# One softmax per query tile, more copies on ScalarE, and a new order of pieces in a gated cross-attention and local-attention block

## The chip, the cores and the metric

The kernel runs on one core of a Trainium2 chip. The metric is device time in microseconds, the median of several runs; lower is better. The core has five instruction queues that run side by side: TensorE (PE) for matmuls, VectorE (DVE), ScalarE (ACT), GpSimd (POOL), and SyncE (SP), which issues transfers. Each queue runs its own instructions in order. Where one needs what another queue produces, it waits on a semaphore.

## The reference

The input is `x` of shape (8, 256, 128): eight sequences of 256 tokens, 128 wide. First comes a gated cross-attention to a context of the same shape (16 heads of 8), then six layers on the residual stream, then a second gate. All arithmetic is in float32.

```python
x = x + tanh(g_xattn) * xattn(layernorm(x), ctx, ctx)      # 16 heads of 8, softmax over 256 keys
h = layernorm(x)
for i in range(6):
    h = attn_layer(shift_tokens(h), Wqkv[i], q_scale[i], k_scale[i], Wo[i]) + h
    h = ffn_layer(shift_tokens(h), ln_g[i], ln_b[i], W1[i], b1[i], W2[i], b2[i]) + h
x = x + tanh(g_ffn) * h

# attn_layer: 16 heads of 64
q, k, v = split(x @ Wqkv)
q, k = l2norm(q) * qs, l2norm(k) * ks
q = q*cos*scale + rotate_half(q)*sin*scale ;  k likewise with 1/scale
# windows of 32 queries see their own 32 keys and the 32 before: 64 keys
sim  = where(mask, -max, q k^T * 8)
attn = softmax(sim) ;  out = (attn @ v) @ Wo

# ffn_layer
xn = (x - mean) / sqrt(var + 1e-5) * g + b
a, gate = split(xn @ W1 + b1) ;  return (a * gelu(gate)) @ W2 + b2
```

## The kernel before

**Tiling.** A sequence is two tiles of 128 tokens on the 128 partitions. `st[b]` is the residual stream of sequence b, features on partitions and tokens along the row, with one column in front for the token shift. There are 6 x 8 = 48 passes through `sequence(k, l, b)`, k = 8 l + b, layer after layer.

**One pass.** Queries and keys of the two tiles make four *chunks* c (CHUNKS: tile 0 key, tile 0 query, tile 1 key, tile 1 query), each in two halves of 512 columns. For each half, `project` (L544, `proj{c}{half}`) does the matmul into a PSUM tile `pj`; `square` (L552, `sq`) on ScalarE writes squares for the norm; `rotate` (L560, `rot`) on VectorE multiplies `pj` with the cosine and sine tables. `squares_sum` (L569, `ss`) sums the squares; `rotate_add` (L575, `radd`) on GpSimd adds the two rotated halves; `norms` and `norms_inverse` (L583 to L591, `norms`, `ninv`) make inverse norms; `normalize` (L598, `nrm`) on GpSimd applies them; `qk_transpose` (L608, `pqt`) and `qk_evacuate` (L616, `qe`) turn queries and keys. Values go by `v_project` (L623, `vp`) and `v_evacuate` (L631, `ve`).

`scores` (L644, `sc{t}{i}`) gives a [128, 16 heads, 64 keys] tile of tile t in PSUM. The softmax works on *groups* of eight heads: four groups, each in two parts. `maxima` (L660, `mx`) does one fused operation per head: mask added, negative minimum taken, result to SBUF. `exponentials` (L670, `ex`) does one activation per head, with the maximum as bias and the row sum accumulated. `sums_inverse` (L679, `rs`) and `divide` (L685, `div`, on GpSimd) finish a group. `p_transpose` (L703, `pt`), `p_evacuate` (L712 and L714, `pe{t}{x}`, on VectorE but for the one piece named in `P_ON_SCALAR`) and `corners` (L720, `co`) turn the probabilities. `attend` (L741) multiplies with the values in two phases, `at` and `aw`; `between` (L752, `av`) is a small VectorE read that lets phase 1 start only when phase 0 is complete. `o_evacuate` (L755, `oe`), `o_project` (L764, `wo`) and `o_add` (`oadd`) end the attention.

The feed-forward half: `f_transpose` (L777, `ftr`), `f_stats` (L194 to L197, `fst`: statistics, then variance plus epsilon), `f_rstd` (L201, `frs`, a power on GpSimd), `f_norm` (L205, `fno`), `f_back` (L793, `fba`), `f_affine` (L798, `faf`), `f_up` (L813; `fga` for the gate half, `fva` for the value half), `f_gelu` (L820, `fge`), `f_gate` (L826, `fgt`), `f_down` (L837, `fdo`) and `f_add` (`fad`).

**The cross-attention** (`cross(b)`, pieces whose names begin with x) runs once per sequence, ahead of that sequence's first layer and beside the layers of earlier sequences. `stats_of` and its epsilon step serve it too.

**What sets the order.** There is no scheduler. Each piece is recorded with a time, `k * SLOTS + PLAN[piece]` with SLOTS = 5; all pieces of all passes are sorted by that time and emitted in that order, and that is the order of every queue. The pieces of one pass have times from 0 to 22.6, so the pieces of some five passes lie interleaved, and after the start the same order repeats for every k. `CROSS_SHIFT` moves each cross block.

```python
    def at(k, piece, fn, *args):
        time = PLAN[piece] if isinstance(piece, str) else piece
        pieces.append((k * SLOTS + time, len(pieces), fn, args))
```

**Buffers.** PSUM has three pools of two buffers each: `ps_p` (tiles pj, pv, px and the cross tiles of tag "pj"), `ps_s` (pqt, scores s, ppt2, po, the gate tile pga) and `ps_m` (ppt1, pa, pw, pxt). In SBUF, the squares tile `sq` has one buffer, the rotation product `ur` two, `u` four. A tile that is read by two engines is read by them one after the other, in the order of the pieces.

**Transfers.** SP loads the weights of a layer in one piece (`load`), long before they are used, with two buffers, so a layer's weights arrive while the layer before runs; `load_vectors`, the inputs of the cross blocks and the results are the other transfers. ScalarE issues a few small ones at the start.

## Time and profile before

| | |
|---|---|
| runs | 1791.76 us median of 3 (1790.74 to 1793.51) |
| profiled execution | span 1786.5 us, TensorE clock 0.996 |
| DVE, slice by slice (tenths) | 3 5 4 6 6 6 8, then 9 to the last two slices |
| ACT, slice by slice | 3 3 4 3 4 5 8, then 9 |
| POOL, slice by slice | 3 0 2 2 3 3 6, then 6 to 7 |
| transfers | 26.32 MB, mean 15 GB/s; the 16 engines are 5.3% busy |
| chain that ended last | PE 74%, DVE 17%, ACT 4%, issue 3% |

In the groups of the profile a row gives line, engine, operation, output and input by the program's names, shapes and count; behind the first bar the busy time and the mean ns of one; behind the second the idle time of that engine in front of these instructions and who ended it. Consecutive instructions of one engine overlap a little, so a mean is longer than the distance from start to start, which a timeline shows.

Two stretches can be told apart. Up to some 300 us the cross blocks run, and no engine is full. After that the six layers repeat one pattern to near the end.

Some rows that the change touches:

| line | what | count | mean ns |
|---|---|---|---|
| L660 | masked minimum of one head, 128x64, DVE | 1536 | 213, and 80 to read the result |
| L670 | exponential of one head, 128x64, ACT | 1536 | 342, and 195 to read the sum |
| L679 | reciprocal of 8 sums, DVE | 192 | 195 |
| L685 | division of 8 heads, 128x512, POOL | 192 | 1043 |
| L712 | probability copy 128x512, DVE | 192 | 678 |
| L714 | probability copy 64x1024, DVE and ACT | 48 each | 1206 and 1010 |
| L798 | affine step, 128x256, DVE | 48 | 529 |
| L197 | variance plus epsilon, 128x2, DVE | 64 | 792 |

### The profile page before, as it was taken

Reading aid. Unit: us, or ns where it says so; the run is one execution under the profiler, and the core shown is the slowest. Engines: PE = TensorE matmul, PEld = TensorE weight load, DVE = VectorE, ACT = ScalarE, POOL = GpSimd, SP = SyncE. Lnnn points to the kernel's source line nnn. Section 1 sums busy time; section 2 is a strip of 40 time slices with the busy share of each in tenths; the row PEclk is TensorE's granted clock in tenths of the full one; section 3 lists DMA queues with packets and bytes.
Section 4 is the critical chain, followed back from the end, with each engine's and each line's share of the span. In section 5 each row is a group of like instructions: output and inputs, shape, how many; then the busy total and the mean of one; then the engine's idle time right before and its main releaser. Section 6 shows DMA issues by size and latency. Waiting matters only on the chain.

```text
span 1786.5 us, 78168 instructions
## 1 busy us (share of the span) xinstructions
PE 1724.5 (97%) x32948; PEld 1135.2 (64%) x32948; DVE 1558.6 (87%) x5314; ACT 1487.5 (83%) x4692; POOL 1092.7 (61%) x716
## 2 busy tenths in 40 slices
PE   7999898999999999999999999999999999999997
PEld 4565455666666666666666666666666666666665
DVE  3546668999999999999999999999999999999974
ACT  3343458999999999999999999999999999998984
POOL 3022336767767676776767677676766767676651
PEclk9999999999999999999999999999999999999999
DMA  3000002000011000010000110000100000000000
GB/s 95 7 13 7 7 2 69 3 3 3 3 38 34 3 3 3 3 51 21 3 3 3 39 34 3 3 3 4 50 23 3 3 3 3 3 6 7 6 9 11
DMA packets 34716, 26.32 MB, mean 15 GB/s; under 512 B 16058, under 2 KB 31294, under 8 KB 34366
## 3 DMA queue, kind: packets, MB, share of 16 engines
q1 hardware_dynamic: 33214, 21.20, 4.1%
q8 instruction: 259, 4.24, 1.0%
q14 instruction: 91, 0.75, 0.1%
q10 hardware_dynamic: 1152, 0.14, 0.1%
HBM read 20.28 MB, written 1.05 MB: 12 GB/s over the span
## 4 chain that ended last, share of the span: by engine, by line
PE 74%; DVE 17%; ACT 4%; issue 3%; POOL 0%; DMA 0%; POOLq 0%; ACTq 0%; DVEq 0%
PE pj L544 17%; PE m L764 9%; PE pv L623 9%; PE po L741 8%; PE s L644 7%; PE s L813 5%; PE pw L837 4%; PE pqt L608 4%; DVE ur L560 4%; PE ppt L703 3%; PE pssT L329 3%; DVE x_max L309 3%; DVE squares L569 3%; DVE rstd L197 2%; PE pa L813 2%
## 5 line engine op out<-in xcount | busy, mean ns | idle before, releaser
L598 POOL TENSOR_TENSOR u<-u,rn 128x1024 f32<-128x1024 f32 x192 | 361.3, 1903 | 283.3 <-DVE rn L591 283.3
L575 POOL TENSOR_TENSOR u<-ur 128x1024 f32<-128x1024 f32 x192 | 451.3, 2362 | 127.4 <-DVE ur L560 98.3
L670 ACT ACTIVATE pr<-pr,nmax 128x64 f32<-128x64 f32 x1536 | 513.1, 342 | 0.6
L544 PE MATMUL pj<-w_qkv,st 128*128 128x512 f32 x768 | 409.4, 615 | 5.1 <-ACT x_big L355 2.2
L552 ACT ACTIVATE sq<-pj 128x512 f32<-128x512 f32 x384 | 227.9, 594 | 89.7 <-PE pj L544 66.7
L670 ACT ACTIVATION_READ_ACCUMULATOR pr<-pr,nmax 128x1 f32 x1536 | 299.2, 195 | 0.0
L560 DVE TENSOR_TENSOR ur<-pj,rotk 128x1024 f32<-128x1024 f32 x192 | 234.9, 1224 | 67.7 <-ACT sq L552 60.9
L685 POOL TENSOR_TENSOR pr<-pr,rs 128x512 f32<-128x512 f32 x192 | 198.2, 1043 | 102.6 <-DVE rs L679 102.6
L660 DVE CUSTOM_DVE_ANT_0 pr<-s,mask 128x64 f32<-128x64 f32 x1536 | 234.4, 213 | 14.0 <-PE s L644 10.8
L560 DVE TENSOR_TENSOR ur<-pj,rotq 128x1024 f32<-128x1024 f32 x192 | 231.4, 1205 | 9.9 <-ACT sq L552 8.5
L569 DVE TENSOR_REDUCE squares<-sq 128x16 f32<-128x1024 f32 x192 | 232.2, 1210 | 0.7
L623 PE MATMUL pv<-w_qkv,st 128*128 128x512 f32 x384 | 215.7, 643 | 0.0
L764 PEld LDWEIGHTS m<-oT,w_o 128*128 128x128 f32 x768 | 145.6, 190 | 58.9 <-issue 43.5
L544 PEld LDWEIGHTS pj<-w_qkv,st 128*128 128x128 f32 x768 | 132.7, 189 | 78.0 <-issue 36.5
L764 PE MATMUL m<-oT,w_o 128*128 128x256 f32 x768 | 181.7, 380 | 0.0
L741 PEld LDWEIGHTS po<-prT,v 64*64 64x64 f32 x6144 | 130.4, 133 | 72.4 <-DVE ur L560 33.4
L644 PE MATMUL s<-kT,qT 64*32 64x64 f32 x12288 | 166.0, 224 | 6.6 <-issue 3.6
L608 PEld LDWEIGHTS pqt<-ident,u 64*128 64x128 f32 x3072 | 110.4, 139 | 80.2 <-issue 68.4
L644 PEld LDWEIGHTS s<-kT,qT 64*32 64x32 f32 x12288 | 134.2, 105 | 39.7 <-issue 20.4
L741 PE MATMUL po<-prT,v 64*64 64x96 f32 (+1 forms) x6144 | 149.1, 240 | 1.4 <-DVE prT L712 1.4
L631 ACT COPY v<-pv 128x512 f32<-128x512 f32 x192 | 112.5, 586 | 44.4 <-PE pv L623 44.1
L608 PE MATMUL pqt<-ident,u 64*128 64x64 f32 x3072 | 136.4, 228 | 0.3 <-DVE x_max L309 0.3
(116 smaller groups left out, 2817.4 us busy)
## 6 DMA issues: line engine op xcount, KB each, us to landing
w_qkv<-in_L_ffn_Wqkv SPq DMA_DIRECT2D x18, 512.0 KB, 6.5
w_o<-in_L_ffn_Wo SPq DMA_DIRECT2D x6, 512.0 KB, 4.0
w<-in_L_ffn_W SPq DMA_DIRECT2D x6, 341.0 KB, 3.0
xin<-in_x SPq DMA_DIRECT2D x8, 128.0 KB, 2.7
cin<-in_ctx SPq DMA_DIRECT2D x8, 128.0 KB, 2.3
out<-res SPq DMA_DIRECT2D x8, 128.0 KB, 1.8
w<-in_L_ffn_W SPq DMA_DIRECT2D x12, 64.0 KB, 2.0
rotq<-in_c_cos_q SPq DMA_DIRECT2D x6, 64.0 KB, 3.4
```

Source lines behind the costliest of these rows:

```text
L544: nc.tensor.matmul(pj, st[b][:, t * P : (t + 1) * P], w["qkv"][:, o : o + 512], start=True, stop=True,)
L560: nc.vector.tensor_tensor(ur[:, :, half * 512 : (half + 1) * 512].rearrange("p x (h d) -> p x h d", d=DH), pj.unsqueeze(1).to_broadcast([P ...
L569: nc.vector.tensor_reduce(squares[k % 2][:, t, i, :, 0], c_.pop(("sq", c)), AX.X, ALU.add)
L575: nc.gpsimd.tensor_tensor(u.rearrange("p h (two d) -> p h two d", two=2), ur[:, 0], ur[:, 1, :, ::-1, :], ALU.add,)
L598: nc.gpsimd.tensor_tensor(u, u, rn, ALU.mult)
L608: nc.tensor.transpose(pt[:, h, j, :], uf[rows, j * P : (j + 1) * P], ident[rows, rows])
L623: nc.tensor.matmul(pj, st[b][:, t * P : (t + 1) * P], w["qkv"][:, o : o + 512], start=True, stop=True,)
L644: nc.tensor.matmul(pss[n * WIN : (n + 1) * WIN, par, c, :], c_["qT"][rows, c, o : o + WIN], c_["kT"][rows, c, k0 : k0 + KEYS], start=True, ...
L660: nc.vector.tensor_tensor_reduce(probabilities(t)[:, par * NPAIR + c, :], c_["pss", t][:, par, c, :], mask[:, t, :], -1.0, 3e38, ALU.add, ...
L670: nc.scalar.activation(pr[:, col, :], pr[:, col, :], AF.Exp, bias=c_.pop(("nmax", g, c)), scale=-1.0, accum_out=c_["sums", t][:, col : col ...
L741: nc.tensor.matmul(po[par * DH : (par + 1) * DH, x, i, q0:q1], v[rows, t, h * DH : (h + 1) * DH], prT[rows, column[h], 64 * half : 64 * ha ...
L764: nc.tensor.matmul(pm, weights[l]["o"][:, c, :], oT[:, c, :], start=(first and c == 4 * half), stop=(not first and c == 4 * half + 3),)
```

## The change

1. The layers' softmax works on one query tile with all 16 heads at a time, in six operations: `masked` (VectorE, scores plus mask from PSUM to SBUF), `maxima` (VectorE reduction), `subtract` (GpSimd), `exponentials` (ScalarE, one activation of 128x1024), `sums_inverse` (VectorE reduction and reciprocal), `divide` (GpSimd). The pieces are called ma, mx, sub, ex, rs, div, each with t = 0 and 1.
2. `P_ON_SCALAR` names all six probability copies, so they run on ScalarE.
3. The LayerNorm's affine step and the addition of epsilon run on ScalarE.
4. PLAN has new times for all pieces of the passes and of the cross blocks, and new CROSS_SHIFT. In three places (`rot01`, `rot11`, `rot30`) the rotation of a projection now stands before its square; `pj` is no longer popped by `rotate` for that reason. The loads keep their times, and the times of `scale_bias`, `clear` and `scale_tables` get names of their own.

```diff
-CROSS_SHIFT = [0.0000000, -1.8673571, -3.6163960, -4.9323222, -6.8028984, -8.5383167, -10.3450958, -11.8335433]
-LOAD_FIRST, LOAD_AFTER, LOAD_AFTER_CROSS = -17.1923263, 20.96, -18.88
-P_ON_SCALAR = {(0, 0)}
+CROSS_SHIFT = [-0.8036217, -2.3498031, -3.8942305, -5.4451205, -6.9040521, -8.3883736, -9.8516719, -9.8386715]
+P_ON_SCALAR = {(t, x) for t in range(NT) for x in range(3)}
...
+    eps = const.tile([P, 1], F32, name="eps")
+    nc.gpsimd.memset(eps, EPS)
...
-        nc.vector.tensor_scalar(rstd, mv[:, :, 1], EPS, None, ALU.add)
+        nc.scalar.activation(rstd, mv[:, :, 1], AF.Identity, bias=eps)
...
-            pj = c_.pop(("pj", c, half))
+            pj = c_["pj", c, half]
...
-        def maxima(g, i):
-            t, par = GROUPS[g]
-            for c in range(4 * i, 4 * i + 4):
-                nmax = small.tile([P, 1], F32, tag="nmax", name="nmax", bufs=24)
-                c_["nmax", g, c] = nmax
-                nc.vector.tensor_tensor_reduce(
-                    probabilities(t)[:, par * NPAIR + c, :], c_["pss", t][:, par, c, :],
-                    mask[:, t, :], -1.0, 3e38, ALU.add, ALU.min, nmax,
-                )
...
-                nc.scalar.activation(
-                    pr[:, col, :], pr[:, col, :], AF.Exp,
-                    bias=c_.pop(("nmax", g, c)), scale=-1.0,
-                    accum_out=c_["sums", t][:, col : col + 1],
-                )
...
+        def masked(t):
+            pss = c_.pop(("pss", t)).rearrange("p a c k -> p (a c) k")
+            nc.vector.tensor_tensor(
+                probabilities(t), pss,
+                mask[:, t, :].unsqueeze(1).to_broadcast([P, HEADS, KEYS]), ALU.add,
+            )
+        def maxima(t):
+            top = c_["top", t] = small.tile([P, HEADS], F32, tag="top", name="top")
+            nc.vector.tensor_reduce(top, probabilities(t), AX.X, ALU.max)
+        def subtract(t):
+            pr = probabilities(t)
+            top = c_.pop(("top", t)).unsqueeze(2).to_broadcast([P, HEADS, KEYS])
+            nc.gpsimd.tensor_tensor(pr, pr, top, ALU.subtract)
+        def exponentials(t):
+            pr = probabilities(t)
+            nc.scalar.activation(pr, pr, AF.Exp)
+        def sums_inverse(t):
+            rs = c_["rs", t] = small.tile([P, HEADS], F32, tag="rs", name="rs")
+            nc.vector.tensor_reduce(rs, probabilities(t), AX.X, ALU.add)
+            nc.vector.reciprocal(rs, rs)
+        def divide(t):
+            pr = probabilities(t)
+            rs = c_.pop(("rs", t)).unsqueeze(2).to_broadcast([P, HEADS, KEYS])
+            nc.gpsimd.tensor_tensor(pr, pr, rs, ALU.mult)
...
-            nc.vector.tensor_scalar(
-                xnT, c_.pop("pxt").rearrange("p n t -> p (n t)"),
-                ln_g[:, l : l + 1], ln_b[:, l : l + 1], ALU.mult, ALU.add,
+            nc.scalar.activation(
+                xnT, c_.pop("pxt").rearrange("p n t -> p (n t)"), AF.Identity,
+                scale=ln_g[:, l : l + 1], bias=ln_b[:, l : l + 1],
             )
```

Since one period is five units of PLAN, the times modulo 5 give the order that every period repeats. The new order of the pieces that the prediction speaks of, queue by queue (a prime marks a piece of the following pass):

```
PE   at0 at1 aw0 aw1 | proj11 | sc10 sc11 | pqt1 | fdo | proj10 | wo0 wo1 | vp00 | proj20 | pqt0 pqt2 | ftr |
     proj21 | pt0 | sc00 sc01 | pqt3 | vp10 | fba | proj30 | proj31 | fga | pt1 | proj01' | vp01 | fva | proj00' | vp11
DVE  av0 av1 ninv ss0 rot11 ma1 mx1 rot10 rs0 fad ss1 oadd rot20 fst rs1 rot21 fno ss2 ma0 mx0 rot30 rot31 ss3
     rot01' co fgt rot00'
ACT  oe0 oe1 sq11 ex0 qe10 sq10 qe11 ex1 ve00 sq20 qe00 qe01 qe21 qe20 fst(eps) sq21 pe00 pe02 qe31 qe30 ve10 faf
     pe01 sq30 fge sq31 pe12 pe10 pe11 sq01' ve01 norms ve11 sq00'
POOL nrm1 nrm0 nrm2 sub1 radd0 div0 nrm3 frs radd1 div1 radd2 radd3 sub0
```

TensorE's order in a period of the kernel before, in blocks by output: px, ppt, pv, pqt, s, pj, pxt, pqt, s, pj, pv, s (up), ppt, pv, pj, s and pa (up), pj, po, pw, pj, po, s, pj, m, s, pqt, pv, pj, m, pj, pqt.

More of the change, by code (lines that the diff above doesn't have):

```diff
@@ L115, in at @@
     def at(k, piece, fn, *args):
-        time = PLAN[piece] if isinstance(piece, str) else piece
+        time = PLAN[piece]
         pieces.append((k * SLOTS + time, len(pieces), fn, args))
@@ L924, in load @@
         layers[l] = load_layer(l)
[L926 to L929 removed]
+    at(0, "ld0", load, 0)
+    at(0, "ld0", load_vectors)
+    at(0, "scb", scale_bias)
+    at(0, "clr", clear)
     for b in range(B):
         cross(b)
[L932 removed]
     for l in range(DEPTH):
[L934 to L937 removed]
+        at(l * B, "tab", scale_tables, l)
+        if l == 1:
+            at(B - 1, "ld1", load, l)
+        elif l:
+            at((l - 1) * B, "ldn", load, l)
         for b in range(B):
```

48 lines of the change are left out of this document (12 added, 36 removed), and 77 rows, old and new, of the table PLAN.

## The prediction

> **What bounds the kernel now.** I read the page first, then the busy time of each engine by stretches, then the timelines of one period, the waits, and the groups by shape.
>
> ```profile
> PE 1724.5 (97%) x32948; PEld 1135.2 (64%) x32948; DVE 1558.6 (87%) x5314; ACT 1487.5 (83%) x4692; POOL 1092.7 (61%) x716
> PE   7999898999999999999999999999999999999997
> ```
> ```profile
> 744.00:806.00 62.00, 61.61 (x1274) 40.73 (x1273) 59.43 (x210) 57.14 (x186) 43.20 (x26) 1.00 0.13 43
> ```
>
> The second fence is one stretch of 62 us: PE 61.61 us busy, PEld, DVE 59.43, ACT 57.14, POOL 43.20, clock 1.00. Three engines are nearly full, and TensorE has no room at all. A faster VectorE or ScalarE can bring nothing here; only TensorE's own order, or a new wait in its queue, moves the time.
>
> ```profile
> 317.10 0.41 PE L777 MATMUL px<-ident,st 128*128 128x128 f32 x2
> ...
> 756.14 0.44 PE L777 MATMUL px<-ident,st 128*128 128x128 f32 x2
> ...
> 787.49 0.44 PE L777 MATMUL px<-ident,st 128*128 128x128 f32 x2
> ...
> 1697.78 0.44 PE L777 MATMUL px<-ident,st 128*128 128x128 f32 x2
> ```
>
> L777 runs once for each of the 48 sequence-layers. Start to start is 31.36 us, and 44 such periods lie between 317.10 and 1697.78. So the span is 317.1 (head) + 44 x 31.36 + 88.7 (tail) = 1786.5. I price the change per period, then head and tail.
>
> ```profile
> 746.06 0.79 PE s L644 x53
> 746.85 1.05 PE pj L544 x2
> ...
> 752.12 0.86 PE pj L544 x2
> ...
> 755.60 0.61 ACT sq L552
> 756.21 0.02 issue
> 756.24 1.23 DVE ur L560
> ```
>
> This is the chain of waits. A wide matmul costs 0.86 us, but 1.06 behind a block of narrow ones: each step from narrow to wide costs 0.20. And the rotation (L560) starts only when the square (L552) of the same projection is done; the waits say so 94 times:
>
> ```profile
> DVE ur L560 <- ACT sq L552: 69.4, 94, 8.4
> PEld pv L623 <- DVE ur L560: 34.1, 45, 0.8
> ```
>
> The second line is the other half: pj, pv and px share two PSUM buffers, so a projection waits until both readers of an earlier one are done.
>
> ```profile
> L560 DVE TENSOR_TENSOR ur<-pj,rotk 128x1024 f32<-128x1024 f32 x192 | 234.9, 1224 | 67.7 <-ACT sq L552 60.9 <-ACT pr L670 0.5 <-issue 0.3
> L569 DVE TENSOR_REDUCE squares<-sq 128x16 f32<-128x1024 f32 x192 | 232.2, 1210 | 0.7
> L598 POOL TENSOR_TENSOR u<-u,rn 128x1024 f32<-128x1024 f32 x192 | 361.3, 1903 | 283.3 <-DVE rn L591 283.3
> L820 ACT ACT_TABLE_LOAD x47 | 60.3, 1283 | 0.8
> ```
>
> These are the rows that price the new operations.
>
> **The change, as busy time per period.** All from start to start in the timelines. VectorE loses 32 masked minima (four in 0.57 us: 4.6), four reciprocals (0.6), five probability copies (4 x 0.60 + 1.13 = 3.5), the epsilon (0.93) and the affine step (0.46): 10.1. It gains two masks, two maxima, two sums and two reciprocals. None stands in the trace; a mask is nearest to L560 (PSUM in, 128x1024: 1.22), a reduction to L569 (1.21), a reciprocal of 16 columns to L368 (0.25, 0.13 where the next does not wait): 7.6. Bounds: half (a 128x512 reduction, L309, took 0.68) and 10% above. ScalarE loses 32 exponentials (four in 1.33: 10.6) and gains two of 128x1024 (L340, 1.05), five copies (4 x 0.50 + 0.92), affine (0.47, L820's shape) and epsilon (0.27, L583): 5.8. GpSimd gains two subtractions (L598's form, 1.90; at most L575's 2.36) and changes four divisions of 1.04 into two of 1.90: +3.4, to some 25 us. So VectorE goes from 29.7 to 27, ScalarE from 28.6 to 24; GpSimd is nowhere full. The sums say "relief" and decide nothing: what counts is order.
>
> [...] In this trace L569 took 1210 ns and the elementwise L560 1224 on as many elements, so the row decides and I charge no penalty.
>
> **TensorE's own order.** The work is the same; a period falls from 32 blocks to 26, and the steps from narrow to wide from eight to five: -0.60. The stall at L793 (L544 before it took 1.29 from start to start, not 0.86) would go too: -0.43. Without waits a period would be 31.36 - 1.03 = 30.3 us.
>
> **The new waits.** I followed the new piece order queue by queue. Pieces are named as in PLAN. Three pairs now run rotation first (rot01, rot11, rot30), the rest square first, and each second reader waits for the first. Two places cannot hide:
>
> (a) ScalarE's order is sq30, gelu (fge), sq31; vp01 needs proj31's buffer, which is free after rot31, which waits for sq31. From the end of proj30: rot30 1.22, sq30 0.64, table load 1.29, gelus 1.11, sq31 0.60, rot31 1.25 = 6.1 us. TensorE has proj31, fga, pt1, proj01 in between: 0.86 + 1.29 + 1.13 + 1.06 = 4.3. It stands for 1.8 us at least. Behind it, ss3, rot01 and then sq01 must end before proj00: 2.9 us against vp01 and fva, 0.2 + 0.86 + 1.29: another 0.6.
>
> (b) VectorE's order is rot00, av0. rot00 waits for sq00, which ScalarE runs behind ve11, which waits for vp11, TensorE's last piece before at0. From vp11's end: 0.53 + 0.60 + 1.17 + 0.16 + 0.05 = 2.5 us until aw0 may start; at0 and at1 cover 1.47. It stands 1.0 us. Before, av0 came straight behind the gate (L826) and did not wait.
>
> VectorE's queue then makes (a) worse. The whole loop, from the end of proj10 to the next: sq10 0.64; VectorE without a gap rot10 1.14, sum 1.37, fad 0.87, ss1 1.13, oadd 0.87, rot20 1.14, statistics 0.90, sum 1.37, rot21 1.14, fno 0.64, ss2 1.13, mask and maximum 2.38, rot30 1.22 = 15.30, at 15.94. (proj30 was ready at 14.0, by TensorE's pieces, so rot30 is 0.7 late.) Then sq30 to rot31 4.89, at 20.83; ss3 1.05, rot01 1.22, sq01 0.63, at 23.73; proj00 with its exposed load 1.08, vp11 0.86, at 25.67; (b) 2.51, at 28.18; aw0 and aw1 1.47; proj11 1.06, scores 1.58, pqt1 0.64, fdo 1.49, proj10 0.86, at **35.28**. That is +3.92 a period: 44 x 3.92 = +172.5.
>
> In the trace a table load takes 1283 ns (L820) and the first gelu starts 1.30 us after it began. [...]
>
> **Covered.** Subtractions and divisions: sub1 can start at -0.5 on the loop's clock, and in GpSimd's order radd0, div0, nrm3, frs end at 3.8, 5.7, 7.6, 9.1; pt0 wants div0 at 8.3, fno frs at 9.9. If that cover (0.8) goes, fno and all behind it slip one for one. Epsilon on ScalarE hides behind the second sum and rot21; affine ends at 13.8, fga starts at 14.9; the copies of pt1 end at 21.7, at0 starts at 25.7. Weight loads keep their places in SP's queue; scb, clr and tab move by pieces, on queues with room in the head.
>
> **Head and tail.** The cross part gets a new order, with pssx between pssT and pox; one cross block spans 28.6 us now, of which 8.9 are maxima that could hide. Bounds: -40 (five us of each of eight) to +16 (the loop's loss in four early sequences); I take -5. The tail has no projections, so (a) is gone: 0, within -5 and +8.
>
> Sum: 1786.5 + 172.5 - 5 = 1954; the runs' median stands 5.3 above the profiled span, so **1959 us**.
>
> **Rivals.**
> 1. *Fixed waits only* (chance 0.17): VectorE's new operations cost less, so rot30 and rot20 start when their inputs are there. The loop loses 0.7 + 0.25: 34.3, and the time is 1786.5 + 44 x 2.94 - 5 + 5.3 = 1916. For it: half-size rows at 0.68; against it: full-size rows all at 1.2.
> 2. *VectorE slowed* (0.13): GpSimd is busy more of the time beside it; 10% on its 20 us in the loop gives 37.3 and 2047. Against it: these rows were taken with GpSimd at 70%.
> 3. *The relief wins* (0.12), faster: square and rotation do not hold each other in the places named, and TensorE runs at 30.3: 1786.5 - 44 x 1.03 - 5 + 5.3 = 1741. It decides where the path from proj30 to rot31 takes under 4.3 us rather than 6.1, and that from vp11 to av0 under 1.5 rather than 2.5. For it: fewer steps from narrow to wide; against it: 94 waits of L560 for L552.
> 4. Gains and waits cancel (0.03): 1792.
>
> **How the numbers follow.** The forecast has 0.55, by itself 1925 to 2000. With rivals 1 and 2 the range is 1890 to 2050; it leaves out rivals 3 and 4 and the ends, under 0.2. About 0.2% is what the measurement can tell: faster 0.12, same 0.02, slower 0.86.
>
> **What would show it.** Right: TensorE's share falls to some 87%, the period of the f_transpose line is near 35.3, v_project waits for ur and the attention matmuls for seen; sq is followed by a table load, three gelus, sq. Wrong: a TensorE still 97% busy with a period near 30.3; or large waits elsewhere (GpSimd's divisions before the transposes); or VectorE idle long before rot30, which is rival 1.

## The result, and the profile after

The changed kernel takes **2067.23 us** (median of 4 runs, 2061.27 to 2073.06) against 1791.25 us (1788.42 to 1793.51): a ratio of 1.1544, 95% interval 1.1515 to 1.1572. The direction was right, the size was not: 1959 us were forecast, and the range ended at 2050.

The page of the kernel after, busy time and TensorE's row of the span:

```profile
PE 1762.0 (85%) x32948; PEld 1168.2 (57%) x32948; DVE 1442.1 (70%) x2082; ACT 1281.9 (62%) x2068; POOL 1257.3 (61%) x717
PE   5899888888888888888888888888888888888887
```

TensorE went from 97% to 85%, and no other engine is over 70%: the engines wait for each other. The f_transpose line (L769 now) gives the period again, from the timeline of after:

```profile
323.60 0.44 PE L769 MATMUL px<-ident,st 128*128 128x128 f32 x2
...
1974.30 0.44 PE L769 MATMUL px<-ident,st 128*128 128x128 f32 x2
```

(1974.30 - 323.60) / 44 = **37.52 us** a period, where 35.28 was forecast. The head is 323.6 (312.1 forecast), the tail 2067.1 - 1974.3 = 92.8 (88.7 forecast). The miss is 44 x 2.24 = 98.6 from the loop, 11.5 from the head, 4.1 from the tail, and -5.1 because these runs stand 0.1 above the profiled span and not 5.3. Together that is 109 us, and 108 were measured: the prediction's 44 x 31.36 is 0.9 short of the 1380.7 us between its two rows.

Busy time by engine in the 44 periods, by stretches, after and then before (length, PE, PEld, DVE, ACT, POOL, granted clock):

```profile
323.60:1974.30 1650.70, 1413.22 (x28091) 941.64 (x28089) 1213.41 (x1681) 1083.78 (x1718) 1108.61 (x583) 0.96 0.03 10
```
```profile
317.10:1697.80 1380.70, 1371.31 (x28091) 910.56 (x28089) 1315.87 (x4628) 1272.79 (x4138) 957.11 (x583) 1.00 0.04 12
```

VectorE and ScalarE are relieved nearly as priced: 102 and 189 us less in the loop, where 44 x 2.5 = 110 and 44 x 4.8 = 211 were said. TensorE has the same 28091 matmuls, but is busy 42 us longer, at a clock of 0.96. It is idle for 237.5 us, 5.4 a period; before, it was idle for 9.4 us in the whole loop. The waits of TensorE, after (sum, times, longest):

```profile
PE pv L622 <- DVE ur L559: 87.4, 44, 2.6
PE po L733 <- DVE seen L744: 46.6, 45, 1.2
PE s L641 <- issue: 46.0, 48, 1.8
PE pj L543 <- DVE ur L559: 31.8, 42, 1.1
...
PE pqt L607 <- issue: 14.3, 14, 1.6
```

v_project for the rotation, attention for `seen`: the two places of the prediction. "issue" is idle time in which nothing is waited for that the profile shows; it stands in the run of scores and in the transposes pqt behind them, some 60 us in all, and the prediction had nothing there. One period of TensorE's timeline, after:

```profile
822.10 0.90 PE L641 MATMUL s<-kT,qT 64*32 64x64 f32 x40 [1.34 <-issue]
...
834.51 1.12 PE L622 MATMUL pv<-w_qkv,st 128*128 128x512 f32 x2 [1.63 <-DVE ur L559]
...
837.45 1.13 PE L543 MATMUL pj<-w_qkv,st 128*128 128x512 f32 x2 [0.53 <-ACT sq L551]
...
841.94 1.55 PE L733 MATMUL po<-prT,v 64*64 64x96 f32 x64 [1.03 <-DVE seen L744]
...
856.78 1.13 PE L543 MATMUL pj<-w_qkv,st 128*128 128x512 f32 x2 [0.76 <-DVE ur L559]
```

These are vp01, proj00, aw0 and proj21, with the gap in the scores ahead of them. The chain of waits, after, in front of vp01 (start, length, what):

```profile
828.29 1.24 DVE ur L559
...
829.61 0.60 ACT sq L551
...
830.23 1.28 ACT L812
831.51 0.01 issue
831.52 1.19 ACT hid L812 x3
832.71 0.49 ACT sq L551
```

rot30, sq30, table load, three gelus, sq31, as written. And the clock by stretches around the gap at 820.76 (the last figures of a line are clock, DMA share, GB/s):

```profile
820.70:822.10 1.40, 0.06 (x5) 0.00 (x1) 1.40 (x4) 0.51 (x2) 1.40 (x2) 0.94 0.00 0
822.10:825.50 3.40, 3.40 (x58) 2.32 (x59) 2.79 (x3) 1.07 (x2) 3.40 (x2) 0.50 0.03 5
825.50:829.00 3.50, 3.50 (x7) 1.63 (x6) 0.73 (x2) 1.53 (x3) 0.35 (x1) 0.53 0.00 0
829.00:831.00 2.00, 2.00 (x39) 1.27 (x39) 0.52 (x1) 1.37 (x2) 0.00 (x0) 1.00 0.00 0
```

After 1.34 us of idle TensorE runs 6.8 us at half its clock, and v_project takes 2.07 us instead of 1.02. Not every wait has this behind it: after the 1.63 us at vp01 (832.88 to 834.51) the clock stays at 1.00. In the clock record of this profile the 44 periods hold 37 stretches at half clock, 30 of them at one of the 44 waits of vp01 and 7 at a gap in the scores. So three things stand in the loss: waits, a low clock behind many of them, and gaps without a releaser.

### The profile page after: what moved, and what is told of

It reads as the page before. It is cut to its first block, busy times and chain, and to the rows that moved or that the text cites. A ratio compares the mean times of both kernels' runs of the same rounds, so it can differ in the third digit from the quotient of the medians.

```text
span 2067.1 us, 72439 instructions
## 1 busy us (share of the span) xinstructions
PE 1762.0 (85%) x32948; PEld 1168.2 (57%) x32948; DVE 1442.1 (70%) x2082; ACT 1281.9 (62%) x2068; POOL 1257.3 (61%) x717
## 3 DMA queue, kind: packets, MB, share of 16 engines
q8 instruction: 259, 4.24, 0.9%
HBM read 20.28 MB, written 1.05 MB: 10 GB/s over the span
## 4 chain that ended last, share of the span: by engine, by line
PE 42%; DVE 31%; ACT 19%; issue 7%; DMA 1%; SPq 0%; POOL 0%; ACTq 0%; DVEq 0%; POOLq 0%
DVE ur L559 16%; PE pj L543 10%; PE pv L622 7%; ACT sq L551 6%; PE s L641 5%; DVE squares L568 4%; PE po L733 4%; PE pssT L328 3%; DVE rs L673 3%; ACT L812 3%; ACT hid L812 3%; PE pqt L607 2%; PE ppt L695 2%; PE pa L805 2%; DVE x_max L308 2%
## 5 line engine op out<-in xcount | busy, mean ns | idle before, releaser
L543 PE MATMUL pj<-w_qkv,st 128*128 128x512 f32 x768 | 415.2, 633 | 42.7 <-DVE ur L559 31.8
L559 DVE TENSOR_TENSOR ur<-pj,rotq 128x1024 f32<-128x1024 f32 x192 | 235.0, 1224 | 302.2 <-ACT sq L551 236.6
L559 DVE TENSOR_TENSOR ur<-pj,rotk 128x1024 f32<-128x1024 f32 x192 | 231.8, 1207 | 115.1 <-ACT sq L551 112.5
L622 PE MATMUL pv<-w_qkv,st 128*128 128x512 f32 x384 | 231.0, 687 | 89.3 <-DVE ur L559 87.4
L665 POOL TENSOR_TENSOR pr<-pr,top 128x1024 f32<-128x1024 f32 x96 | 182.5, 1901 | 29.2 <-DVE top L660 26.2
L641 PE MATMUL s<-kT,qT 64*32 64x64 f32 x12288 | 156.2, 226 | 47.5 <-issue 46.0
L733 PE MATMUL po<-prT,v 64*64 64x96 f32 (+1 forms) x6144 | 148.0, 240 | 47.0 <-DVE seen L744 46.6
L679 POOL TENSOR_TENSOR pr<-pr,rs 128x1024 f32<-128x1024 f32 x96 | 182.6, 1902 | 6.9 <-DVE rs L674 6.9
L200 POOL TENSOR_TENSOR rstd<-rstd,half_neg 128x2 f32<-128x2 f32 x64 | 45.0, 703 | 225.4 <-ACT rstd L196 103.6
L756 PE MATMUL m<-oT,w_o 128*128 128x256 f32 x768 | 173.5, 379 | 0.0
L615 ACT COPY qT<-pqt 128x512 f32<-128x512 f32 x192 | 106.9, 583 | 89.8 <-PE pqt L607 89.8
L747 ACT COPY oT<-po 128x1024 f32<-128x1024 f32 x96 | 92.5, 1016 | 108.9 <-PE po L733 108.9
L622 PEld LDWEIGHTS pv<-w_qkv,st 128*128 128x128 f32 x384 | 70.4, 205 | 158.4 <-DVE ur L559 124.2
```

Source lines behind the costliest of these rows:

```text
L543: nc.tensor.matmul(pj, st[b][:, t * P : (t + 1) * P], w["qkv"][:, o : o + 512], start=True, stop=True,)
L559: nc.vector.tensor_tensor(ur[:, :, half * 512 : (half + 1) * 512].rearrange("p x (h d) -> p x h d", d=DH), pj.unsqueeze(1).to_broadcast([P ...
L622: nc.tensor.matmul(pj, st[b][:, t * P : (t + 1) * P], w["qkv"][:, o : o + 512], start=True, stop=True,)
L641: nc.tensor.matmul(pss[n * WIN : (n + 1) * WIN, par, c, :], c_["qT"][rows, c, o : o + WIN], c_["kT"][rows, c, k0 : k0 + KEYS], start=True, ...
L665: nc.gpsimd.tensor_tensor(pr, pr, top, ALU.subtract)
L679: nc.gpsimd.tensor_tensor(pr, pr, rs, ALU.mult)
```

## The experiments

All times are medians; the ratio is to the kernel before in runs on the same chip, with its interval. The diffs are of PLAN, against the changed kernel unless said otherwise. The expectations are quoted as written before each run.

### e1 to e4: the waits and the clock

**e1_gelu_last**

```diff
-    "fge": 19.6562344
+    "fge": 19.7200000
```

> Changed kernel with one piece moved: fge (table load and gelus) behind sq31 instead of in front of it, so that rot31 need not wait for them. Theory (waits in the loop, plus a TensorE clock that falls to 0.5 behind the long wait at v_project): the wait of 1.98 us goes, but the three probability copies and sq01 now stand behind the gelus, so the loop shrinks by about 1.5 us, and the clock stays near 1.0, which gives back another 1.2 us: period 37.5 to about 34.8, time about 1950. Rival (only the waits count, the low clock has another cause): 1.5 us a period, about 2000. Second rival (the wait is hidden anyway by another path of the loop): within 15 us of 2067.

Measured: 1951.11 us, 1.0891 (1.0841 to 1.0941). One step of ScalarE moved by one place is worth 116 us; the prediction priced place (a) at 44 x 2.4 = 106. The wait at pv (87.4 us) is gone from TensorE's list and the profiled run's clock is 0.984 instead of 0.959, but proj00's wait for the square grew from 7.4 to 32.6 us. So 116 is a sum of other things than the 106, and that they lie close is partly luck.

**e2_seen_first**

```diff
-    "rot00": 0.8851100
+    "rot00": 1.2500000
```

> Changed kernel with rot00 moved behind av0 and av1, so that the small read that phase 1 of attend waits for no longer stands behind a rotation that waits for sq00. Theory: the 1.03 us wait of the attention matmuls goes from each period and nothing takes its place: 44 x 1.0 = 45 us, about 2020. Rival (VectorE is so late elsewhere that the same time is lost at ma1): no change, 2067.

Measured: 2032.73 us, 1.1347 (1.1294 to 1.1400), 34.5 us less; place (b) was priced at 44 x 1.0 = 44. The wait for `seen` went, but the others stayed, and f_transpose and pqt wait 22 us more than before (px 16.0 instead of 6.1, pqt for u 12.5).

**e3_split_scores**

```diff
-    "sc01": 8.5952106, "ma0": 8.9645606, "mx0": 9.0213562
+    "sc01": 9.2000000, "ma0": 9.2010000, "mx0": 9.2020000
```

> Changed kernel with sc01 (and ma0, mx0 behind it) moved behind pqt3 and vp10, so that the run of narrow matmuls ppt, s, s, pqt is broken. Theory (the gaps inside s that no semaphore ends come from instructions arriving too slowly for a long run of short matmuls): the gaps at this place fall from about 0.9 us to near 0, 30 to 50 us, about 2025. Rival (the gaps follow the instruction count and simply land elsewhere, or come from the clock): same sum of gaps, 2060 to 2075.

Measured: 2115.60 us, 1.1810 (1.1755 to 1.1864): the wrong way. The gaps in the scores fell from 46.0 to 15.0 us, but mask and maximum came later, rot30 behind them on VectorE too, and the wait at v_project grew from 87 to 134 us. It says that the gaps can be moved by the order and nothing of what they cost.

**e4_warm_wait**: a projection that stands just ahead of v_project's wait is computed three times, 1.72 us more of TensorE's work a period, 76 us in 44.

```diff
-            nc.tensor.matmul(
+            for _ in range(3 if (c, half) == (0, 1) else 1):
+                nc.tensor.matmul(
```

> Changed kernel in which the matmul proj01, the last one in front of the long wait at v_project, is done three times over (the result is the same): 1.72 us more work a period on TensorE, put into its wait of 1.98 us. Theory (that wait makes the clock fall to 0.5, which then costs 1 to 1.5 us of each period): the clock rises towards 1.0 and the time falls, by some 50 us to about 2015. Rival (the clock does not follow this wait): the time is the same or up to 20 us longer, 2067 to 2090.

Measured: 2040.20 us, 1.1393 (1.1352 to 1.1433). **27 us less time with 76 us more work**, about half of the gain expected. The clock of the profiled run is 0.993 instead of 0.959, and 1.00 in its loop (326.85 to 1937.00) instead of 0.96; the wait at v_project fell to 13.0 us in all. So the added matmuls fill time that was waited anyway, and the clock was higher with them. The gaps in the scores are nearly as long as without them (43.6 and 46.0 us), so in this run they did not go with the low clock.

### e5 to e8: order or operations?

**e5_waits_undone** moves what stood in front of each wait:

```diff
-    "fge": 19.6562344, "sq30": 4.4926206, "sq01": 0.2076265, "sq11": 1.5722557
+    "fge": 19.7200000, "sq30": 4.4325000, "sq01": -0.0600000, "sq11": 1.5090000
-    "rot00": 0.8851100, "sq00": 0.8586334, "norms": 5.4142825, "rs0": 12.4370536
+    "rot00": 1.2500000, "sq00": 0.7358000, "norms": 5.7359000, "rs0": 12.3800000
-    "pe12": 14.7317162, "pe10": 14.8841584, "pe11": 14.9695499, "proj21": 3.4013131
+    "pe12": 15.0100000, "pe10": 15.0200000, "pe11": 15.0300000, "proj21": 3.5000000
```

> The changed kernel with the seven steps moved that the trace of the changed kernel names in front of a TensorE wait: the gelu goes behind the last layer's square sq31, sq30 and sq10's fellows sq01 and sq11 ahead of the rotation next to them, rot00 behind the second copy of the attention's result, the third probability copies behind sq01, the sums of tile 0 ahead of rot10, proj21 one place later. All operations of the change stay. Theory (the waits of the new order and the lower clock that follows them are the loss; the operations are not): the period falls from 37.5 to between 31 and 32 us, granted clock .99 or more, time 1760 to 1820 us. Rival (the new operations themselves, slowed by what runs beside them, set the period): the named waits go, but others come up in their place, and the time stays above 1880 us.

Measured: 1857.92 us, 1.0378 (1.0355 to 1.0402). 209 of the 276 us are back with every operation of the change in place; the time lies between the two ranges given. The period is 32.4 us, just above what was expected, and TensorE now waits at other lines (pqt 0.94, which the trace puts down to the normalised u).

**e6_scalar_load**, the kernel before with one part of the change:

```diff
-P_ON_SCALAR = {(0, 0)}
+P_ON_SCALAR = {(t, x) for t in range(NT) for x in range(3)}
...
-            nc.vector.tensor_scalar(
-                xnT, c_.pop("pxt").rearrange("p n t -> p (n t)"),
+            nc.scalar.activation(
+                xnT, c_.pop("pxt").rearrange("p n t -> p (n t)"), AF.Identity,
```

> The kernel before, its order and its 64 separate softmax operations kept, with the copies, the LayerNorm affine and the eps addition on ScalarE, which is one part of the change alone. ScalarE was busy 28.6 us of a period of 31.36 before, and the copies and the affine put about 3.5 us on it. Theory: ScalarE becomes the bound at about 32.1 us and the time goes to 1810 to 1850 us; VectorE's relief brings nothing. Rival (VectorE bound the old loop, so that relief wins): under 1780 us.

Measured: 1930.00 us, 1.0787 (1.0764 to 1.0811), a period of 34.2: above the range expected, and the rival is out. By stretches, e6 (1000 us of its loop; the fourth busy time is ScalarE's):

```profile
500.00:1500.00 1000.00, 914.21 (x18665) 606.64 (x18663) 744.49 (x2879) 939.99 (x2950) 633.43 (x387) 1.00 0.05 15
```

ScalarE's work is the 32.1 us expected (0.940 x 34.2), but it was not busy without a break: it stood 2 us a period. "Busy time is the bound" gave 0.7 us a period, a quarter of the loss; which waits make the rest was not followed up.

**e7_tile_softmax** (the kernel before with the tile-wise softmax at places among the old ones) and **e8_old_order** (with both parts); of the old steps' times, those of the same names go:

```diff
+    "ma0": 9.1908941, "mx0": 9.3140708, "sub0": 9.6000000, "ex0": 10.4676246, "rs0": 11.6069412,
+    "div0": 12.6559582, "ma1": 11.9964850, "mx1": 12.0338320, "sub1": 12.0500000, "ex1": 12.8447020,
+    "rs1": 14.2388404, "div1": 14.7144398
```

> The kernel before with the tile-wise softmax in six operations put at the places where the sixteen-part one stood, the copies and the affine left on VectorE: the other part of the change alone, in the old order. Theory: TensorE's own order stays, so the period is between 30.3 and 31.4 us, the time 1760 to 1800 us; the softmax as such costs nothing. Rival (the six large operations hold up what queues behind them on VectorE and GpSimd, at 1.2 and 1.9 us each): over 1850 us.

> All new operations of the change in the old order of pieces: the change without its third part. Theory (the order is the loss): 1740 to 1810 us, with no wait of more than 0.5 us a period at v_project. Rival (the operations are the loss, whatever the order): over 1880 us.

Measured: 2312.72 us, 1.2914 (1.2887 to 1.2942), and 2331.46 us, 1.3025 (1.2997 to 1.3053). Both expectations fell. The largest wait, e8 (e7 has 285.2 us of it):

```profile
PE ppt L701 <- POOL pr L685: 289.1, 91, 6.2
```

The probability transposes wait for GpSimd's division, twice a period, and the granted clock of the two profiled runs is 0.871 and 0.868. Six operations on a whole tile are a chain of 1.2 + 1.2 + 1.9 + 1.05 + 1.45 + 1.9 = 8.7 us in which one waits for the other; in the kernel before, a tile's softmax was split into groups and parts that could overlap. Only one set of places among the old steps was tried. So the new order was not the mistake beside a good change: the new softmax needs a new order, and the one it got has its own waits.

### e9 and e10: the head, and the gaps without a releaser

**e9_late_load**

```diff
-    "ld0": -17.1923263
+    "ld0": -14.4800000
```

> The changed kernel with one step moved: the load of the first layer's weights (ld0) goes behind the second load of x on SP's queue, where the kernel before had it. The prediction said that the weight loads keep their places; in the trace of the changed kernel the second x tile is issued at 23.8 us instead of 4.0, the statistics on VectorE wait 10.6 us for it, and x_max behind them makes TensorE wait 9.2 us at pssx. Theory: that wait goes, the first f_transpose starts at 313 to 318 us instead of 323.6, the time falls by 6 to 10 us to 2057 to 2061 us. Rival (the head's loss comes from the new order of the cross part): the head stays at 322 us or more, the time at 2067 us.

Measured: 2057.58 us, 1.1485 (1.1453 to 1.1516), 9.7 us less. What happened in the changed kernel is in three queues, SP's, VectorE's and TensorE's timelines, after:

```profile
23.82 1.30 SPq L216 DMA_DIRECT2D xin<-in_x  x1
```
```profile
26.91 0.29 DVE L193 BATCH_NORM_STATS2 stats<-xin 128x6 f32<-128x128 f32 x1 [10.60 <-DMA xin<-in_x]
```
```profile
28.47 2.67 PE L298 MATMUL pssx<-xk,x_big 32*128 32x256 f32 x12 [9.16 <-DVE x_max L308]
```

The second x tile is issued at 23.82 us (4.00 before), behind a whole layer's weights; the statistics wait for it, the maxima queue behind the statistics, TensorE behind the maxima. In e9 the first f_transpose starts here:

```profile
314.24 0.44 PE L769 MATMUL px<-ident,st 128*128 128x128 f32 x2
```

**e10_shifted_stream**: 64 matmul instructions more, once, ahead of the first period.

```diff
-            for c in range(4 * i, 4 * i + 4):
+            for c in 2 * [*range(4 * i, 4 * i + 4)] if (k, t, i) == (0, 0, 0) else range(4 * i, 4 * i + 4):
```

> The changed kernel with 64 matmul instructions more, once, ahead of the first period (the first scores of the first sequence are computed twice). In the changed kernel each gap inside the run of scores matmuls that no semaphore explains ends 1.2 to 1.5 us after a 16 KB packet of TensorE's instructions has landed, and the gaps stand 127 matmul instructions, or a multiple, apart. Theory (TensorE runs out of instructions): the gaps move by 64 matmul instructions along the run, so that near 820 us of the span the gap that stood behind the 87th of the 128 scores stands near the 23rd (or in the transposes or copies next to them); the time stays within 25 us of 2067. Rival (the gap belongs to the work, a buffer or a semaphore that the trace doesn't show): it stays where it was.

Measured: 2057.17 us, 1.1491 (1.1464 to 1.1519). The runs of scores in two periods that follow each other, TensorE's timeline, after, and the same two periods in e10:

```profile
744.92 1.15 PE L641 MATMUL s<-kT,qT 64*32 64x64 f32 x95
747.37 0.48 PE L641 MATMUL s<-kT,qT 64*32 64x64 f32 x33 [1.29 <-issue]
...
782.40 1.14 PE L641 MATMUL s<-kT,qT 64*32 64x64 f32 x92
784.64 0.62 PE L641 MATMUL s<-kT,qT 64*32 64x64 f32 x36 [1.11 <-issue]
```
```profile
734.73 0.45 PE L641 MATMUL s<-kT,qT 64*32 64x64 f32 x31
736.34 1.50 PE L641 MATMUL s<-kT,qT 64*32 64x64 f32 x97 [1.16 <-issue]
...
772.32 0.44 PE L641 MATMUL s<-kT,qT 64*32 64x64 f32 x28
773.39 1.20 PE L641 MATMUL s<-kT,qT 64*32 64x64 f32 x100 [0.62 <-issue]
```

Behind 95 and 92 scores in the one, behind 31 and 28 in the other: exactly 64 earlier. In these periods the gap went with the count of matmuls and not with the work. From period to period it comes 3 earlier; a period has 638 matmuls, and five times 127 are 635. Counted along the whole stream of the changed kernel, these gaps stand at place 84 to 93 of 127 from the first period to the last. In e10 the scores at 809 and 830 us have no gap (all 128 run in one piece); the time fell by 10 us.

The DMA view of the changed kernel, 819 to 823.5 us, in 40 slices of 0.11 us, with the instruction queue's line:

```profile
GB/s 0 0 0 0 0 146 0 0 0 0 0 0 0 0 0 0 0 0 0 0 0 0 0 0 0 0 0 0 0 0 0 0 0 0 0 0 0 0 0 0
...
q8 instruction: 1, 0.02, 1.5%
```

One packet, issued at 819.6, 1.1 us long (1.5% of 16 x 4.5); the scores stop at 820.76 and go on at 822.10, 2.5 us after its start. All 54 gaps of this kind over 0.3 us in the 44 periods end 2.2 to 2.9 us after a packet's start. On the page this queue has 259 packets with 4.24 MB, 16.4 KB each; TensorE's 2 x 32948 matmuls and weight loads divided by 259 are 254, or 127 matmuls with their weight loads, the distance at which the gaps come back. That TensorE stands there for want of its instructions is my reading of this agreement in time and count; no run shows it directly.

### e11 to e18: can the new operations run level?

Each of these mends what the trace of the one before it names; all contain e5 and the late load of e9. The diffs are against the version that each builds on: e11 on e5, e12 and e14 on e11, e13 on e14, e16 on e13, e15 and e17 on e16, e18 on e17.

**e11_waits_undone_2** and **e12_split_scores_2** (the second and third pair of lines are e12's alone)

```diff
-    "ninv": 6.3896942, "ld0": -17.1923263
+    "ninv": 6.2400000, "ld0": -14.4800000
-    "proj21": 3.5000000
+    "proj21": 3.5600000
-    "fdo": 21.8928788
+    "fdo": 21.6100000
```

> e5_waits_undone with two more steps moved: the inverse of the norms (ninv) ahead of rot00 on VectorE, since in e5 pqt waits 0.94 us a period for the normalised u behind it, and ld0 as in e9_late_load. Theory: the pqt wait goes and half of it or more is gained, 20 to 40 us a run, and 6 to 10 us of the head: 1812 to 1835 us. Rival (rot00 later by the 0.83 us of ninv makes a projection wait in its place): 1845 us or more.

> e11_waits_undone_2 with a wide step put between the two halves of each tile's scores (proj21 between sc00 and sc01, f_down between sc10 and sc11), so that TensorE's stream has no run of more than about 130 narrow matmul instructions. No work is added and no mask is made later by more than one f_down. Theory (the gaps of 0.6 us in the scores and 0.35 us in the transposes are TensorE waiting for its instructions): most of 0.5 to 0.9 us a period is gained over e11, 20 to 40 us: 1780 to 1810 us, not above the kernel before by more than 1%. Rival (the gaps only move to another place, or the later halves delay the masks): no gain over e11.

Measured: 1848.95 us, 1.0326 (1.0304 to 1.0349), and 1895.63 us, 1.0590 (1.0568 to 1.0612). e11 gained what the load step is worth, and its period stayed at 32.4, with the wait of pqt turned into a gap of 0.98. ScalarE's and TensorE's timelines, e11, show what ends it:

```profile
829.80 0.60 ACT L551 ACTIVATE sq<-pj 128x512 f32<-128x512 f32 x1 [1.61 <-DVE squares L568]
830.30 1.01 ACT L747 COPY oT<-po 128x1024 f32<-128x1024 f32 x1
```
```profile
831.40 0.71 PE L607 MATMUL pqt<-ident,u 64*128 64x64 f32 x16 [0.98 <-issue]
```

The second copy of the attention's result (oe1) empties the buffer of `ps_s` that pqt1 takes, and ends 0.09 us before pqt1 starts. It is late because e5 put the square sq11 ahead of it, which waits for the sum of squares. In e5 it ends 0.10 us before pqt1 too (847.77 and 847.87), so the normalised u was not the reason. e12 is slower, and its periods show where: 20 of 32.4 to 32.8, then seventeen of 33.0 to 37.6, then 32.4 again. TensorE's timeline in one of the slow ones, e12:

```profile
1078.41 1.21 PE L695 MATMUL ppt<-ident,pr 32*64 32x32 f32 x64 [0.35 <-POOL pr L679]
1079.55 0.78 PE L641 MATMUL s<-kT,qT 64*32 64x64 f32 x54
1081.96 0.45 PE L641 MATMUL s<-kT,qT 64*32 64x64 f32 x10 [1.64 <-issue]
1082.34 2.07 PE L543 MATMUL pj<-w_qkv,st 128*128 128x512 f32 x2
```

With the projection moved between the scores, 64 transposes and 64 scores stand side by side: 128 matmuls in 2 us. Among them TensorE stood for 1.64 us here, with no releaser in the trace, and the projection behind took 2.07 us instead of 1.02, as v_project did at half clock in the changed kernel (823.98). That the gap came into this run by the drift of 3 a period is my reading; no run shows it.

**e14_gpsimd_order**, and **e13_gpsimd_order_split** (the last two pairs)

```diff
-    "radd0": 2.5164517, "pe12": 15.0100000
+    "radd0": 2.1300000, "pe12": 14.8500000
-    "fdo": 21.8928788
+    "fdo": 21.6100000
-    "pqt3": 8.9645077
+    "pqt3": 8.5600000
```

> e11_waits_undone_2 with two steps moved. e5, e11 and the first 20 periods of e12 have the same period of 32.4 us although TensorE waits at different lines: a loop through GpSimd holds it (rn, three normalisations, sub1, radd0, div0, then the transposes pt0, then TensorE up to the attention result, seen, rn). radd0 goes ahead of sub1, into the 1 us in which GpSimd waits for the maxima, so that div0 ends 0.9 us earlier; and the copy pe12, for which pa waits 0.5 us, goes ahead of the square next to it on ScalarE. Theory: the period falls to 31.3 to 32.0 us, the time to 1795 to 1830 us. Rival (another loop, or the instruction stream, sets 32.4): 1840 us or more.

> e14_gpsimd_order with the narrow runs of TensorE broken up by existing steps: f_down between the halves of tile 1's scores, the transposes of chunk 3 (pqt3) between those of tile 0. Theory (the gaps that no semaphore explains are TensorE waiting for its instructions, and cost 0.3 to 1.2 us a period): 10 to 45 us below e14, between 1765 and 1800 us, that is within 1.5% of the kernel before on either side. Rival (with the other waits gone the gaps lie inside slack, or only move): within 8 us of e14, or above it.

Measured: 1849.77 us, 1.0315 (1.0285 to 1.0344), and 1827.38 us, 1.0187 (1.0155 to 1.0219). e14 missed: 32.3, no better than e11, so GpSimd's order did not hold 32.4. e13 gains 22 us over e14 with the same work, by the places of two steps, and its idle time without a releaser at scores and pqt is 41 us instead of 74. This does not show that the instruction stream was the reason: the gaps in the scores fell from 29 to 14 us, but those at pqt keep their place in the period (in e14 at place 106, 109, 112, 115 of 127 in periods that follow each other), and in e14 the copy oe1 ends 0.10 us before them (836.11 and 836.21), as in e11. The two steps of e13 are those that let f_down fill this wait. Its absolute size was expected lower; pqt3, now early, stands 0.83 us.

**e16_early_pqt** and **e15_early_pqt_vp10** (the last two pairs)

```diff
-    "pqt0": 7.8124841, "qe00": 7.9304226, "qe01": 8.0850087
+    "pqt0": 7.7000000, "qe00": 7.8700000, "qe01": 7.8800000
-    "pqt3": 8.5600000, "vp10": 14.1980336
+    "pqt3": 8.5100000, "vp10": 13.5850000
-    "frs": 18.6267239, "fno": 18.8288715
+    "frs": 18.5900000, "fno": 18.6000000
```

> e13_gpsimd_order_split with the first chunk's transposes (pqt0) and their copies ahead of proj20, since in e13 the probability transposes wait 0.31 us a period and start as ScalarE's second kT copy ends. Theory (that wait and the fetch gap next to it go): period 31.7 to about 31.2 to 31.4 us, time 1800 to 1820 us. Rival (the later sq20 and rot20 make proj21 wait instead): 1825 us or more.

> e16_early_pqt with vp10 between the halves of tile 0's scores, pqt3 ahead of them, and the LayerNorm's xn (whose reading frees vp10's buffer) ahead of rot21 on VectorE. In e13 TensorE has a gap of 0.83 us in front of pqt3, after ppt64, a projection and 64 scores. Theory (instruction stream): the gap goes, the period is 30.6 to 31.0 us, the time 1765 to 1800 us, the kernel before or a little below it. Rival (vp10 waits for xn in the place of the gap, or tile 0's mask comes too late): 1815 us or more.

Measured: 1817.79 us, 1.0156 (1.0121 to 1.0190), and 1839.19 us, 1.0275 (1.0236 to 1.0314). e16's time is in its range, but its period did not fall (31.8, the mean of the first 40, in both): the gain lies in the last four periods (135.5 us in e13, 128.7 in e16) and outside the loop, so the reason given for it isn't shown. e15 fell to its rival: the scores then wait 0.94 us for ScalarE's copy of the probabilities. The same copy is behind the 0.83 of e16; TensorE's and ScalarE's timelines, e16:

```profile
835.43 0.71 PE L607 MATMUL pqt<-ident,u 64*128 64x64 f32 x16 [0.83 <-POOL rstd L200]
```
```profile
834.34 0.99 ACT L706 COPY prT<-ppt 64x1024 f32<-64x1024 f32 x1
```

The trace names GpSimd, but its operation is a power of two columns that pqt doesn't read; the copy ends 0.1 us before pqt starts, and empties the buffer that pqt takes. The place of this gap moves by 3 from period to period (54, 57, 60 of 127), whereas the gaps of the changed kernel moved from 93 to 84 in all 44 periods.

**e17_early_copy** moves that copy, **e18_late_maximum** (the last pair) one operation more:

```diff
-    "pe00": 13.8368814, "fst": 18.4090969
+    "pe00": 13.4320000, "fst": 18.4330000
-    "mx0": 9.0213562
+    "mx0": 10.0700000
```

> e16_early_pqt with the copy pe00 ahead of the statistics step fst, so that ScalarE makes it right after tile 0's transposes (it is idle there for 1.2 us) and not behind the square sq21. Theory (pqt3 waits for the buffer that pe00 empties): the 0.83 us go, the period falls from 31.75 to 30.9 to 31.2 us, the time to 1776 to 1800 us, level with the kernel before or a little below it. Rival (the gap is the instruction stream's, or GpSimd's as named): 1812 us or more.

> e17_early_copy with tile 0's maximum (mx0, 1.2 us) behind rot01 on VectorE. In e17 the wait went from pqt3 to proj00, which waits 0.74 us for rot01 at the end of 12 us of VectorE without a gap, and the period stayed at 31.7. GpSimd's subtraction, which needs the maximum, has 1.4 us of idle ahead of it. Theory (only waits of the order are left; the operations cost nothing of themselves): the 0.74 us go, the period is 30.9 to 31.2 us, the time 1775 to 1800 us, within 0.6% of the kernel before. Rival (VectorE, now with 27 us of work in a period of 31, has no room and the wait turns up at the next rotation or at the attention): 1810 us or more.

Measured: 1814.41 us, 1.0131 (1.0109 to 1.0153), and **1787.13 us, 0.9985 (0.9974 to 0.9997)**. In e17 the wait of pqt3 is gone as said, but the period stayed at 31.7, with 0.74 us now at proj00, which waits for rot01. In e18 that went too: most periods are 30.9 us. The page, TensorE's longest waits, and its loop by stretches, e18:

```profile
PE 1715.0 (96%) x32948; PEld 1136.2 (64%) x32948; DVE 1431.1 (80%) x2082; ACT 1263.0 (71%) x2068; POOL 1258.5 (70%) x717
```
```profile
PE pn L315 <- DVE x_max L308: 5.3, 6, 1.6
PE s L641 <- issue: 4.8, 13, 0.7
```
```profile
320.00:1692.00 1372.00, 1360.37 (x28101) 908.02 (x28099) 1201.58 (x1680) 1065.30 (x1719) 1111.03 (x585) 1.00 0.04 12
```

Every operation of the change is in e18, and it runs level with the kernel before: its interval ends just below 1, by less than the 0.2% that this kernel's measurement can tell. So the 276 us were the order of the steps: 24 of PLAN's times differ between the changed kernel and e18. In the profiled runs its 44 periods are shorter than those of before (31.10 us in the mean, 326.67 to 1695.05, instead of 31.38), and its head is longer (326.7 us instead of 317.1); what the head of e18 waits for was not followed up.

## Why the prediction was wrong in size

- **What bounds it**: right. TensorE's queue and new waits in it decided, VectorE's and ScalarE's relief nothing. 85% stands against the forecast 87%, but busy time and period both grew, so the share hides the miss.
- **The prices of the new operations**: right. Subtraction 1.90 us and division 1.90, exponential 1.06, mask 1.22, maximum 1.22, sum 1.20 and reciprocal 0.25. Rival 2 (VectorE slowed by GpSimd, 2047 us) came nearest to the time, but its mechanism isn't there: the rotation takes 1224 and 1207 ns, not 10% more.
- **The waits**: the places were right. vp01 "for 1.8 us at least" and late by 0.7 more: 1.99 a period (87.4 / 44). aw0 1.0: 1.04. proj00 0.6: 0.53 in the period shown, but only 14 waits in all, 7.4 / 44 = 0.2 a period. Divisions and subtractions were covered as said: TensorE's list has no wait of the probability transposes for them. proj21's 0.76 (it waits for rot20, whose buffer it takes) was not named. All of TensorE's stalls were forecast at 35.28 - 30.3 = 5.0 a period; those at a semaphore measure (87.4 + 46.6 + 31.8 + 7.4) / 44 = 3.9.
- **The step that failed: "at 35.28"**. The loop was summed as if TensorE, where it doesn't wait for a semaphore, ran at its full clock and without a gap. In its place stand, per period: work 30.9 (e18's busy time, 1360.37 / 44, where I had 30.3; the stretch is 3.6 us longer than 44 of its periods, under 0.1 each); the same work at a lower clock, (1413.22 - 1360.37) / 44 = 1.2; waits 3.9; gaps without a releaser (46.0 + 14.3) / 44 = 1.4. Sum 37.4 of the 37.52. In e4 the time fell by 27 us with the clock at 0.993 instead of 0.959, and in e10 the gaps went with the count of matmuls, 64 earlier. So the forecast loop of 35.28 had 5.0 of stalls where 3.9 came, and lacked 0.6 of work, 1.2 of clock and 1.4 of gaps. How the 98.6 us divide between them is this sum's reading; the causes feed each other, and no run took away the low clock or the gaps alone. The two orders differ at the place of the gaps: in the loop of before the runs of ppt, s and pqt hold 80 matmuls at most, and its scores have 3.6 us of such gaps in the whole span; the new order has ppt64, s128 and pqt16 in one run, and 46.0 us. Of the clock the profile of before says nothing: it stands at 1.00 in a loop with 9.4 us of idle time.
- **"Without waits a period would be 30.3 us"**: 0.6 too low, going by the 30.9 of e18, whose order differs from the change's in places.
- **"Weight loads keep their places in SP's queue"**: wrong, and the larger part of the head's miss. ld0 kept its time of -17.192, but the second load of x, at 5 - 20.330 - 1.867 = -17.197 before, went to 5 - 19.487 - 2.350 = -16.837 and so behind it. e9: 9.4 us of the head. By these two profiles the cross part's new order is worth 314.2 - 317.1 = -2.9, where I had taken -5; that is not shown, since the heads of e11 to e18, with the same late load, lie between 320.4 and 329.6.
- **The table load**: right. The first gelu starts 1.29 us after the load began (830.23 to 831.52), as it was priced.
- **The tail**: +4.1, inside its bounds.

## What to carry to other kernels

Price a new wait on TensorE with its consequence: what the clock does behind it (0.96 here, instead of 1.00), and what the longer path makes late next; the sum of stalls alone was 2.2 us of 37.5 too short here, although it had the waits themselves too long. When an order is rearranged, look at every queue for what has moved past a step that kept its own time, and count how many narrow matmuls now stand side by side (here 208 instead of 80 at most, with gaps of up to 1.8 us in the scores). And before a softmax of many small parts is made one of few large ones, compare the length of its chain with the time that the order leaves between scores and transposes: the same operations gave 2331, 2067 and 1787 us in three orders.

## What the runs showed of the hardware

- **The clock was low behind many short waits, but not behind each.** In the changed kernel 1.34 us of idle (820.76 to 822.10) were followed by 6.8 us at half clock, 1.63 us (832.88 to 834.51) by none. In its clock record the 37 falls in the loop stand whole multiples of 3.413 us apart, and the clock stays at half for 3.41 us (33 times) or 6.83 (4 times). The 3.41 us ahead of a fall held 1.0 to 2.6 us of idle, but some others with 1.5 to 1.9 us had no fall behind them; so the idle time does not decide alone, and what else does was not shown. Adding 76 us of work in front of a wait made the kernel 27 us faster, with the clock of the profiled run at 0.993 instead of 0.959 (e4).
- **Gaps without a releaser went with the count of matmuls.** In the changed kernel 54 such gaps over 0.3 us, the longest 1.8, stand in the scores and in pqt; they lie at place 84 to 93 of 127 and end 2.2 to 2.9 us after the start of a packet of 16.4 KB on the instruction queue. With 64 matmuls more ahead of them they came 64 earlier, and two later runs of 128 scores had none (1.4 us from 808.98 to 810.40, e10). In e12 the same order gave 20 periods of 32.4 to 32.8 us and then seventeen of 33.0 to 37.6.
- **The releaser that the trace named was the wrong one** where a buffer was the reason: e16's pqt was put down to GpSimd, e11's to nothing at all, and in both a copy of ScalarE ended 0.1 us before; with the copy moved (e17), that wait of pqt, 31.7 us in e16, is no longer among TensorE's longest. The place in the count told such a gap from the others: those of the changed kernel moved from 93 to 84 in 44 periods, that of e16 by three a period (54, 57, 60).
